# Eight shifted copies of 64 lags for the Toeplitz rows, and blocks of q*v 56 rows apart

## The chip, the core and the metric

The kernel is one program on one core of a Trainium2 chip. Its time is the device time of one execution in microseconds (us), and lower is better. The core has five engines that take instructions in order, each from a list of its own: TensorE (PE in the profile, with its weight loads as PEld), VectorE (DVE), ScalarE (ACT), GpSimd (POOL) and SyncE (SP), which here issues transfers only. Sixteen DMA engines move data between device memory (HBM) and the on-chip SBUF. A transfer is issued by an instruction on SP, ACT or POOL and runs beside the computation.

## The reference

The input is `x`, 8 images of 56 x 56 positions with 192 channels, float32. Four layers each add something to it. Layers 0 and 1 are the ones that the change touches:

```python
p = silu(x @ p_w.T + p_b)          # x after a group norm; D1 = 576 channels
q = silu(x @ q_w.T + q_b)
v = silu(x @ v_w.T + v_b)
qv = q * v
o1 = _toeplitz(qv.reshape(b * h, w, D1), a1)     # along the rows
o2 = _toeplitz(transpose(qv), a2)                # along the columns
out = (p * (o1 + o2)) @ o_w.T + o_b
```

`_toeplitz` multiplies every line of 56 positions, channel by channel, with a 56 x 56 Toeplitz matrix, whose 111 coefficients (one for each lag) come from a small network of the lag times a decay that depends on the channel. Layer 2 is a ConvNeXt block and layer 3 is attention in windows; the change leaves both alone.

## The kernel before, in words

**Passes.** The images are handled in pairs and fours: `qvs` holds two HBM tensors, one for images 0, 1 and 4, 5 and one for the rest. For each layer and each of them there is a q/v pass (`tno_qv`, called Q: normalise on ACT at L246, 128 x 256 matmuls at L263, bias add on VectorE at L272, SiLU on ACT at L301, product on GpSimd at L304, store of the product to `qv` by SP at L307), a Toeplitz pass (`tno_toeplitz`, called TZ) and an output pass (`tno_out`, called O: loads of the sums `s` at L508 and of `x` at L119, matmuls at L536 to L592).

**Layout of qv.** A block holds 32 channels of four images: 56 x 56 positions with 128 values each, the four images of a channel side by side. Before the change a block has room for 64 rows of 56 positions; the last 8 rows are zeros, written once by two transfers of GpSimd's queue at L743.

**Coefficient tables.** `decay_tables` (L136) works out the 111 coefficients of each channel, in chunks of 128 channels. For each chunk a tile `a` (L191) holds them in reverse order with zeros behind, and SP writes them to an HBM table as shifted copies (L204): row g of the table holds, for 32 channels, the lags from 4g on. With `TG, TW = 16, 60` there are 16 such copies of 60 lags. A Toeplitz step reads its coefficient tile `tm` from them with four transfers (L393), each filling every fourth partition: partition 4g + k gets the g-th copy shifted by k more. That yields 64 partitions for each of the two blocks of the step, each shifted by one lag from the one above. The matmul then takes 32 consecutive lags as its weights.

**Toeplitz steps.** Each TZ runs 18 steps n, in pairs: `blk, d = divmod(n, 2)`. A step works on two blocks (64 channels), along rows where d is 0 and along columns where d is 1. Its `q` tile is 128 partitions of 56 x 128 values, two buffers. For d = 0 it comes by two transfers (L380) that put the position within the row on the partitions, one of them on ACT's queue; for d = 1 it comes by one transfer (L383), which takes 128 rows of 28672 bytes as they stand, the rows of zeros among them. The matmuls of L406 use 56 partitions of each half. ACT copies the results out (L413), VectorE transposes and adds (L424, L426), GpSimd adds (L429) and stores sums of finished blocks (L436, L444). The loads of step n + 2 are issued after the last group of step n.

**Order of the work.** `tno_layers` (L681) starts with a table stage, in which the statistics of the input, the first Q and the tables of both layers alternate. Then four TZ passes follow, each woven by `weave` (L644) with a lane of Q and O work: whenever the lane has done its share, the next part of a TZ step is issued. PE, ACT, DVE and POOL run in the order in which the program is written; the order on SP's queue is set by the framework. `tm` has two tiles, the products that wait to be stored have three buffers (`tp`, `bufs=3`), and `x` tiles of `input_stats` have seven (L215).

Of the kernel before, what the change touches and what calls it, by code (L numbers as in the profile page):

```python
# [12 lines left out]
F32 = mybir.dt.float32  # L13
# [13 lines left out]
B, H, W, C = 8, 56, 56, 192  # L27
T = H * W
HALF = [slice(0, 64), slice(64, 128)]
TT = 448  # L30
NT = T // TT
D1 = 576
# [6 lines left out]
def view(ap, offset, dims):  # L39

    return bass.AP(ap.tensor, ap.offset + offset, [ap.ap[0], *dims])


class Net:
# [86 lines left out]

    TG, TW = 16, 60

    def decay_tables(self, L, p, tables):  # L136

        nc, inp = self.nc, self.inp
        tv = p.tile([32, 111], F32, name=f"{L}tv", bufs=1)
        nc.sync.dma_start(tv, inp["tvec"])  # L140
        pows = []
        for c in range(5):
            m = min(128, D1 - 128 * c)
            sl = p.tile([128, 1], F32, name=f"{L}sl")
            nc.sync.dma_start(sl[:m], inp[f"{L}_slope"][128 * c : 128 * c + m, :])
            nc.vector.tensor_scalar(sl[:m], sl[:m], 0.0, 1.0, ALU.max, ALU.min)
            nc.vector.tensor_scalar(sl[:m], sl[:m], 1.0 - 0.95, 0.95, ALU.mult, ALU.add)
            pw = p.tile([128, 64], F32, name=f"{L}pw", bufs=5)
            nc.gpsimd.memset(pw[:m, 0:1], 1.0)
            n = 1  # L150
            while n < 64:
                nc.vector.tensor_scalar(
                    pw[:m, n : 2 * n], pw[:m, 0:n], sl[:m], None, ALU.mult
                )
                n *= 2
                if n < 64:
                    sq = p.tile([128, 1], F32, name=f"{L}sl")
                    nc.vector.tensor_mul(sq[:m], sl[:m], sl[:m])
                    sl = sq
            pows.append(pw)  # L160
            yield 1.0
        for d in range(2):
            t = f"{L}_t{d + 1}"
            w0 = p.tile([32, 2], F32, name="w0")
            nc.sync.dma_start(w0[:, 0:1], inp[f"{t}_w0"])
            nc.sync.dma_start(w0[:, 1:2], inp[f"{t}_b0"])
            ws = p.tile([32, 3, 32], F32, name="ws")
            nc.sync.dma_start(ws, inp[f"{t}_ws"])
            bs = p.tile([32, 3], F32, name="bs")
            nc.sync.dma_start(bs, inp[f"{t}_bs"])  # L170
            wo = p.tile([32, D1], F32, name="wo")
            nc.sync.dma_start(wo, inp[f"{t}_wo"])
            bo = p.tile([128, 5], F32, name="bo")
            nc.sync.dma_start(bo, inp[f"{t}_bo"])
            h = p.tile([32, 111], F32, name=f"{L}h")
            nc.vector.tensor_scalar(h, tv, w0[:, 0:1], w0[:, 1:2], ALU.mult, ALU.add)
            nc.vector.tensor_scalar(h, h, 0.0, None, ALU.max)
            for i in range(3):
                hp = self.bank2()[:32, 0, :111]
                nc.tensor.matmul(hp, ws[:, i, :], h, start=True, stop=True)  # L180
                h = p.tile([32, 111], F32, name=f"{L}h")
                nc.vector.tensor_scalar(h, hp, bs[:, i : i + 1], 0.0, ALU.add, ALU.max)
                yield 1.0
            for c in range(5):
                m = min(128, D1 - 128 * c)
                ap = self.bank2()[:, 0, :111]
                nc.tensor.matmul(
                    ap[:m], wo[:, 128 * c : 128 * c + m], h, start=True, stop=True
                )
                a = p.tile([128, 4 * self.TG + 56], F32, name=f"{L}a")  # L190
                nc.gpsimd.memset(a[:m, 111:], 0.0)  # L191
                back = view(pows[c][:m], 55, [[-1, 55]])
                for lo, hi, dec in ((0, 55, back), (55, 111, pows[c][:m, 0:56])):
                    nc.vector.scalar_tensor_tensor(
                        view(a[:m], 110 - lo, [[-1, hi - lo]]),
                        ap[:m, lo:hi],
                        bo[:m, c : c + 1],
                        dec,
                        ALU.add,
                        ALU.mult,  # L200
                    )
                for n in range(m // 32):
                    to = tables[d][self.TG * (4 * c + n) : self.TG * (4 * c + n + 1)]
                    nc.sync.dma_start(  # L204
                        to.rearrange("g (c w) -> c g w", w=self.TW),
                        view(a[32 * n : 32 * n + 32], 0, [[4, self.TG], [1, self.TW]]),
                    )
                yield 1.0

    def input_stats(self, xs, gn, j, p):  # L210

        nc = self.nc
        st = self.tp.tile([128, 3, 14, 6], F32, name="st", bufs=2)
        for t in range(NT):
            x = p.tile([128, 3, TT], F32, name="x", bufs=7)  # L215
            self.load_pair(x, xs, j, slice(t * TT, (t + 1) * TT))
            for k in range(3):
                nc.vector.bn_stats(st[:, k, t, :], x[:, k, :])
            yield
        self.norms.append(self.pair_gn_finish(st[:, :, :NT], gn, j))  # L220
        for more in self.all_norms():
            pass

    def tno_qv(self, L, j0, xs, gn, qv, apart=None, cols=(0, 2 * D1), g0=0):
# [3 lines left out]
        nc, p, inp = self.nc, self.tp, self.inp  # L228
# [5 lines left out]
        w, bias = self.wq[:, 0:2], self.wq[:, 2]  # L234
# [62 lines left out]
        def multiply(m, n, z, at, c0):  # L297
            k = n // 128
            for f in stores:
                f()  # L300
            nc.scalar.activation(z[:m, :n, :], z[:m, :n, :], AF.Silu)  # L301
            prod = p.tile([128, 4, DC * 4], F32, name="t4")
            half = z[:m, :n, :].rearrange("p (n h c) b -> p n h (c b)", h=2, c=DC)
            nc.gpsimd.tensor_mul(prod[:m, :k], half[:, :, 0], half[:, :, 1])  # L304
            n0 = c0 // 128
            stores[:] = [
                lambda: nc.sync.dma_start(  # L307
                    qv[2 * n0 : 2 * n0 + 2 * k, at : at + m, :].rearrange("n t e -> t n e"),
                    prod[:m, :k].rearrange("p n (h e) -> p (n h) e", h=2),
                )  # L310
            ]
# [7 lines left out]
        if apart:  # L319
            units = []  # L320
            for g in range(2):
                x, t0, n = loaded[g]
                for s in range(0, n, 128):
                    for c0 in range(0, 2 * D1, 512):
                        k = min(512, 2 * D1 - c0)
# [19 lines left out]
        for g in range(2 if apart else g0, groups):  # L345
            x, t0, n = loaded.pop(0)
# [18 lines left out]
    def tno_toeplitz(self, j0, mats, qv, o):  # L365
# [6 lines left out]
        def load(n):  # L372
            blk, d = divmod(n, 2)
            q = p.tile([128, H, 128], F32, name="q", bufs=2)
            if d == 0:

                for half in range(2):
                    of = qv[2 * blk + half, :T].rearrange("(h w) e -> w h e", w=W)
                    by = nc.scalar if half and n > 1 else nc.sync
                    by.dma_start(q[64 * half : 64 * half + W], of)  # L380
            else:
                of = qv[2 * blk : 2 * blk + 2].rearrange("n (h w) e -> (n h) (w e)", w=W)
                nc.sync.dma_start(q.rearrange("p i e -> p (i e)"), of)  # L383
            return q

        def matrices(n):

            blk, d = divmod(n, 2)
            row = 32 * self.TW
            at = mats[d].offset + 2 * blk * self.TG * row  # L390
            for k in range(4):
                of = bass.AP(mats[d].tensor, at + k, [[row, 2 * self.TG], [1, row]])
                nc.sync.dma_start(self.tms[n % 2][k:128:4], of)  # L393

        def along(n, q, ot, g):
# [285 lines left out]
    def tno_layers(self, x0, x1, x2, gn, last):  # L681
# [11 lines left out]
        ]  # L693
        qvs = {

            j0: self.dram.tile([D1 // 32, 64 * W, 128], F32, name=f"qv{j0}") for j0 in (0, 2)
        }
        o = [self.dram.tile([B // 2, 9, 128, T], F32, name=f"{L}_sum") for L in LS]
        x = (x0, x1, x2)
        with ExitStack() as ctx, ExitStack() as wqp:  # L700
# [7 lines left out]
            with tc.tile_pool(name="tab", bufs=2) as tab:  # L708
# [20 lines left out]
                with tc.manual_schedule(engines=ENGINES):  # L729
                    for n in range(28):  # L730
                        next(more, None)
                        if n == 18:
                            next(rest)
                        if next(first, None) is None:
                            next(rest)
                        if n < 21:
                            next(decay[0])
                        if n >= 7:
                            next(decay[1])
                        if n in (14, 21):  # L740
                            qv = qvs[0 if n == 14 else 2]
                            to = qv[:, T:].rearrange("n (p k) e -> p n (k e)", p=112)
                            nc.gpsimd.dma_start(to, view(none, 0, [[0, D1 // 32], [1, 512]]))  # L743
                    for more in decay:
                        assert next(more, None) is None
                lanes = [[(rest, QT * 5 / 9 * 21 / 25 - 25.0), (Q(0, 2), QT)], [(O(0, 0), OT), (Q(1, 0), QT)]]
# [933 lines left out]
```

## Time and profile before

| | us |
|---|---|
| median of 3 runs | 5438.96 |
| lowest and highest run | 5432.41, 5443.45 |
| profiled execution, device time | 5425.63 |
| its span | 5423.8 |
| TensorE busy in the span | 5166.0 (95%) |
| VectorE busy | 2589.3 (48%) |
| ScalarE busy | 2383.5 (44%) |
| GpSimd busy | 1767.2 (33%) |

The median is the time that is compared. All durations below come from the one profiled execution. Its span runs from the first to the last recorded instruction; 1.8 us of its device time lie around the span. Busy shares are averages over the whole span. The table stage lasts from about 100 to 376 us, the woven stages from 376 to about 2970 us, and the later layers follow. A row of a timeline gives the start, the duration, the engine, the line, the operation, the target and source tiles by name, and in brackets the idle time before it and what ended it. In a list of waits each line gives the waiting engine and line, what it waited for, and then total us, times, and the longest.

### The profile page before, as it was taken

How to read it: one execution, taken by the hardware profiler on the slowest of the kernel's cores; microseconds unless marked ns; L12 is line 12 of the kernel's file. 1: busy time of each engine (PE TensorE's matmuls, PEld its weight loads, DVE VectorE, ACT ScalarE, POOL GpSimd, SP SyncE). 2: the span in 40 equal slices, each digit the busy share in tenths (PEclk: the TensorE clock that was granted, in tenths of full speed). 3: DMA queues.
4: the chain of work that ended last, by engine and by line, in shares of the span. 5: the costliest groups of instructions: out<-in, count | busy, mean ns of one | idle time of the engine just before them, and what ended most of it. 6: DMA issues, size and time to landing. Idle time of an engine off the chain costs nothing.

```text
span 5423.8 us, 144350 instructions
## 1 busy us (share of the span) xinstructions
PE 5166.0 (95%) x64672; PEld 3811.2 (70%) x64672; DVE 2589.3 (48%) x3990; ACT 2383.5 (44%) x3179; POOL 1767.2 (33%) x1291
## 2 busy tenths in 40 slices
PE   7879999999999999999999899989999999999998
PEld 4657777777777777777777789856665444777776
DVE  6535556455555555555556422422222331566666
ACT  3345555444554454655455422243323333444443
POOL 2225675133664243546443100000000100333333
PEclk9889999999999999999999999999999999999998
DMA  7699997888786999889897667635454221445552
GB/s 251 151 243 283 289 311 234 265 281 267 241 262 176 307 317 318 279 226 291 285 312 266 205 223 248 229 96 190 135 174 124 75 68 49 85 98 108 101 102 68
DMA packets 1051146, 1116.48 MB, mean 206 GB/s; under 512 B 235200, under 2 KB 986304, under 8 KB 1036128
## 3 DMA queue, kind: packets, MB, share of 16 engines
q1 hardware_dynamic: 911584, 854.88, 52.9%
q0 software_dynamic: 38144, 200.99, 9.6%
q10 hardware_dynamic: 100800, 51.38, 3.9%
q8 instruction: 508, 8.32, 0.6%
q14 instruction: 110, 0.90, 0.1%
HBM read 743.17 MB, written 363.94 MB: 204 GB/s over the span
## 4 chain that ended last, share of the span: by engine, by line
PE 50%; DVE 3%; DMA 3%; issue 1%; ACT 1%; POOL 1%; SPq 0%; POOLq 0%; ACTq 0%; DVEq 0%
PE bank L980 7%; PE bank L837 5%; PE bank L1060 5%; PE bank L1254 4%; PE bank L263 4%; PE bank L592 3%; PE bank L1074 3%; PE bank L536 3%; PE bank L1370 2%; PE bank L1201 2%; PE bank L1284 2%; PE bank L1325 2%; PE bank L406 2%; PE bank L586 1%; PE bank L1344 1%
## 5 line engine op out<-in xcount | busy, mean ns | idle before, releaser
L263 PE MATMUL bank<-wq,t 128*128 128x256 f32 (+4 forms) x7680 | 1290.3, 374 | 72.1 <-DVE t L272 40.8
L263 PEld LDWEIGHTS bank<-wq,t 128*128 128x128 f32 (+2 forms) x7680 | 1005.2, 190 | 350.8 <-issue 92.4
L272 DVE TENSOR_TENSOR t<-bank,wq 128x1024 f32<-128x1024 f32 (+3 forms) x480 | 517.7, 1112 | 692.5 <-PE bank L263 537.1
L304 POOL TENSOR_TENSOR t<-t 128x1024 f32<-128x1024 f32 (+2 forms) x288 | 528.0, 1847 | 676.5 <-ACT t L301 339.1
L413 ACT COPY ot<-bank 128x896 f32<-128x896 f32 x576 | 493.4, 909 | 515.1 <-PE bank L406 401.8
L429 POOL TENSOR_TENSOR s<-s,ot 128x1568 f32<-128x1568 f32 x128 | 551.1, 4306 | 193.8 <-DVE ot L426 128.4
L301 ACT ACTIVATE t<-t 128x2048 f32<-128x2048 f32 (+2 forms) x288 | 423.0, 1488 | 328.8 <-DVE t L272 319.0
L406 PE MATMUL bank<-q,tm 56*32 56x224 f32 x18432 | 504.9, 353 | 22.0 <-DMA tm<-L_tab 10.6
L406 PEld LDWEIGHTS bank<-q,tm 56*32 56x32 f32 x18432 | 340.0, 106 | 148.2 <-issue 81.7
L122 POOL DMA_DIRECT2D x<-t x112 | 87.0, 777 | 1071.7 <-DVE t L601 1007.4
L560 DVE TENSOR_TENSOR t<-t,bank 128x896 f32<-128x896 f32 x224 | 242.8, 1088 | 401.6 <-ACT bank L555 346.0
L555 ACT ACTIVATE bank<-bank,wo 128x448 f32<-128x448 f32 x448 | 262.8, 605 | 377.4 <-PE bank L545 349.8
L980 PE MATMUL bank<-z,w 128*128 128x448 f32 (+1 forms) x1344 | 413.3, 555 | 2.8 <-DVE xt L828 2.8
L536 PE MATMUL bank<-t,wo 128*128 128x224 f32 x1792 | 375.9, 364 | 21.1 <-ACT t L515 10.6
L536 PEld LDWEIGHTS bank<-t,wo 128*128 128x128 f32 x1792 | 337.7, 194 | 51.7 <-issue 29.6
L592 PE MATMUL bank<-t,wo 128*128 128x224 f32 x1792 | 368.9, 359 | 0.0
L592 PEld LDWEIGHTS bank<-t,wo 128*128 128x128 f32 x1792 | 329.9, 190 | 31.1 <-issue 31.1
L980 PEld LDWEIGHTS bank<-z,w 128*128 128x128 f32 (+1 forms) x1344 | 183.0, 189 | 209.8 <-issue 199.5
L837 PEld LDWEIGHTS bank<-xt,cm 113*112 113x112 f32 x3072 | 309.7, 178 | 25.7 <-issue 23.3
L837 PE MATMUL bank<-xt,cm 113*112 113x108 f32 (+2 forms) x3072 | 316.0, 263 | 1.0 <-ACT h L989 1.0
L127 POOL DMA_DIRECT2D x<-x x64 | 36.7, 573 | 855.5 <-DVE x L1011 796.7
L424 DVE STREAM_TRANSPOSE s<-ot 128x1792 f32<-128x1792 f32 x144 | 292.8, 2034 | 24.5 <-ACT ot L413 16.2
(162 smaller groups left out, 6977.2 us busy)
## 6 DMA issues: line engine op xcount, KB each, us to landing
q<-qv SPq DMA_DIRECT2D x36, 3584.0 KB
t<-L_sum SPq DMA_DIRECT2D x112, 1008.0 KB
L_sum<-s POOLq DMA_DIRECT2D x256, 392.0 KB, 7.2
qv<-t SPq DMA_DIRECT2D x192, 512.0 KB
cm<-in_L_cm SPq DMA_DIRECT2D x96, 896.0 KB
tm<-L_tab SPq DMA_DIRECT2D x288, 240.0 KB
q<-qv SPq DMA_DIRECT2D x40, 1568.0 KB
q<-qv ACTq DMA_DIRECT2D x32, 1568.0 KB
```

The source lines that it names most:

```text
L263: nc.tensor.matmul(pp[:m, b, 256 * j : 256 * j + k], x[rows, j, 2 if part else b, s : s + m], w[rows, part, c0 + c : c0 + c + k],  start=p ...
L272: nc.vector.tensor_add(z[:m, c : c + k, :], view(pp[:m], 0, [[1, k], [256, 4]]), view(bias[:m], c0 + c, [[1, k], [0, 4]]),)
L301: nc.scalar.activation(z[:m, :n, :], z[:m, :n, :], AF.Silu)
L304: nc.gpsimd.tensor_mul(prod[:m, :k], half[:, :, 0], half[:, :, 1])
L406: nc.tensor.matmul(pt[32 * j : 32 * j + 32, r, hf * 224 : (hf + 1) * 224], tm[rows, at : at + 32], q[rows, :, 4 * c : 4 * c + 4], start=Tr ...
L413: nc.scalar.copy(view(ot, 4 * (g % 4), [[16, 2], [32, 112], [1, 4]]), view(pt, 0, [[512, 2], [4, 112], [1, 4]]),)
L424: nc.vector.transpose(to, of.rearrange("p (i k) -> p i k", k=32))
L429: add.tensor_add(to, to, view(of, 0, [[1, 28], [32, 56]]))
L536: mm(gs[c // 2][:, b, c % 2 * 256 : c % 2 * 256 + N], pw[:, 0, 128 * c : 128 * c + 128], xn[:, b], start=c % 2 == 0, stop=False,)
L592: mm(P[:, b, :N], ow[:, c, 0:128], g[:, 4 * b + c], start=False, stop=c == 3)
L837: nc.tensor.matmul(pc[:, 128 * e + 4 * m0 : 128 * e + 4 * m1], cm[:113, e, k, :], xt[:, m0 - 1 + k : m1 - 1 + k, c + e, :], start=n == 0 a ...
L980: nc.tensor.matmul(phs[c][:, s, :TT], w0[rows, part, at : at + 128], z[rows, Z[2 if part else s], :], start=part == flip, stop=part != flip,)
```

## The change

The table keeps 8 copies of 64 lags, each shifted by 8, where it kept 16 of 60, shifted by 4. A `tm` tile takes 8 table rows for each 32 channels, and each twice: once from its start and once from 4 lags on, hence `[4, 2]` in the source of L392. The coefficient tiles `a` stay 120 wide (4 x 16 + 56 and 8 x 8 + 56) and have four buffers in place of two. Blocks of `qv` stand 56 rows apart, with no zeros between them; 8 rows of zeros stand at the end of each of the two tensors, since the load of the last block also takes 64 rows. The d = 1 load reads, for each of two blocks that begin 56 rows apart, 64 rows. What it reads beyond 56 isn't used by the matmuls. The `x` tiles of `input_stats` have six buffers in place of seven.

```diff
-    TG, TW = 16, 60
+    TG, TW = 8, 64
...
-                a = p.tile([128, 4 * self.TG + 56], F32, name=f"{L}a")
+                a = p.tile([128, 8 * self.TG + 56], F32, name=f"{L}a", bufs=4)
...
-                        view(a[32 * n : 32 * n + 32], 0, [[4, self.TG], [1, self.TW]]),
+                        view(a[32 * n : 32 * n + 32], 0, [[8, self.TG], [1, self.TW]]),
...
-            x = p.tile([128, 3, TT], F32, name="x", bufs=7)
+            x = p.tile([128, 3, TT], F32, name="x", bufs=6)
...
-                    qv[2 * n0 : 2 * n0 + 2 * k, at : at + m, :].rearrange("n t e -> t n e"),
+                    qv[2 * n0 * T : 2 * (n0 + k) * T].rearrange("(n t) e -> t n e", t=T)[at : at + m],
...
-                    of = qv[2 * blk + half, :T].rearrange("(h w) e -> w h e", w=W)
+                    of = qv[(2 * blk + half) * T :][:T].rearrange("(h w) e -> w h e", w=W)
...
-                of = qv[2 * blk : 2 * blk + 2].rearrange("n (h w) e -> (n h) (w e)", w=W)
+                rows = qv.rearrange("(h w) e -> h (w e)", w=W)[2 * H * blk : 2 * H * blk + H + 64]
+                of = bass.AP(rows.tensor, rows.offset, [[H * W * 128, 2], [W * 128, 64], [1, W * 128]])
...
-                of = bass.AP(mats[d].tensor, at + k, [[row, 2 * self.TG], [1, row]])
+                of = bass.AP(mats[d].tensor, at + k, [[row, 2 * self.TG], [4, 2], [1, row]])
...
-            j0: self.dram.tile([D1 // 32, 64 * W, 128], F32, name=f"qv{j0}") for j0 in (0, 2)
+            j0: self.dram.tile([D1 // 32 * T + 8 * W, 128], F32, name=f"qv{j0}") for j0 in (0, 2)
...
-                            to = qv[:, T:].rearrange("n (p k) e -> p n (k e)", p=112)
-                            nc.gpsimd.dma_start(to, view(none, 0, [[0, D1 // 32], [1, 512]]))
+                            to = qv[D1 // 32 * T :].rearrange("(p k) e -> p (k e)", p=112)
+                            nc.gpsimd.dma_start(to, none)
```

## The prediction

> **What bounds the kernel now.** I read the page's busy shares first, then the waits, then windows of the woven stages, then timelines around single loads. The page:
> ```profile
> span 5423.8 us, 144350 instructions
> PE 5166.0 (95%) x64672; PEld 3811.2 (70%) x64672; DVE 2589.3 (48%) x3990; ACT 2383.5 (44%) x3179; POOL 1767.2 (33%) x1291
> q<-qv SPq DMA_DIRECT2D x36, 3584.0 KB
> tm<-L_tab SPq DMA_DIRECT2D x288, 240.0 KB
> ```
> TensorE is busy for 95% of the span. It is the bound, and a transfer costs time only where TensorE comes to wait for it. The one large transfer that the change rewrites is the `q<-qv` load of L383: 36 of 3584 KB each, on SP's queue.
>
> The list of waits (total, times, longest) says what such loads cost now:
> ```profile
> POOL t L304 <- DMA qv<-t: 306.1, 54, 31.1
> ...
> PE bank L406 <- DMA tm<-L_tab: 10.6, 1, 10.6
> ...
> PE bank L406 <- DMA q<-qv: 3.4, 1, 3.4
> ```
> TensorE waits once for a coefficient tile and once for a `q` tile: both kinds of load are hidden. GpSimd's products already wait 306.1 us for stores of `qv`, so SP's queue is not idle.
>
> Windows: busy time of PE, PEld, DVE, ACT, POOL, then granted clock, mean busy share of the 16 DMA engines, GB/s. In order: all woven stages; the start of one L383 load; the start of the next; attention's `v` loads of L1233; the last `v` load of L1240 alone:
> ```profile
> 376.00:2970.00 2594.00, 2500.34 (x31566) 1945.96 (x31566) 1421.15 (x1393) 1354.29 (x1840) 1233.35 (x764) 0.98 0.86 275
> 1066.00:1075.00 9.00, 8.96 (x125) 6.52 (x124) 5.48 (x4) 5.45 (x9) 7.25 (x6) 1.00 1.06 418
> 1136.00:1145.00 9.00, 8.90 (x125) 6.47 (x124) 5.82 (x4) 4.58 (x8) 7.09 (x6) 1.00 1.09 425
> 4617.50:4618.30 0.80, 0.80 (x24) 0.65 (x16) 0.23 (x1) 0.48 (x1) 0.00 (x0) 1.00 1.02 161
> 4619.10:4619.45 0.35, 0.35 (x20) 0.07 (x8) 0.00 (x0) 0.00 (x0) 0.00 (x0) 1.00 0.21 33
> ```
> The DMA engines are 86% busy over the woven stages. The L383 load, whose source is 128 equal rows, keeps all 16 busy at 418 to 425 GB/s, 26.1 to 26.6 GB/s for each. The last two rows matter most. L1233's source has a leading count of 48 and its loads fill all engines (1.02). L1240's has a leading count of 4 and holds a share of 0.21, 3.4 engines of 16, for the whole 0.35 us. Spread over 16 engines the same packet time would be over in 0.35 x 0.21 = 0.07 us.
>
> Timeline of SP's queue, with the two L383 loads of the rows above, then of TensorE, with the first use of the first of them and two groups of 32 matmuls in the table stage:
> ```profile
> 1065.05 0.44 SPq L383 DMA_DIRECT2D q<-qv  x1
> ...
> 1098.85 0.34 SPq L380 DMA_DIRECT2D q<-qv  x1
> ...
> 1134.80 0.33 SPq L383 DMA_DIRECT2D q<-qv  x1
> ```
> ```profile
> 211.26 0.54 PE L180 MATMUL bank<-L1h,ws 32*32 32x111 f32 x2 [9.74 <-DVE L1h L177]
> 211.74 8.48 PE L263 MATMUL bank<-wq,t 128*128 128x256 f32 x32
> ...
> 282.86 0.54 PE L180 MATMUL bank<-L1h,ws 32*32 32x111 f32 x2 [7.50 <-issue]
> ...
> 294.12 5.65 PE L263 MATMUL bank<-wq,t 128*128 128x256 f32 x32
> ...
> 313.06 3.35 PE L263 MATMUL bank<-wq,t 128*128 128x256 f32 x7 [10.76 <-ACT t L246]
> ...
> 1105.18 1.75 PE L406 MATMUL bank<-q,tm 56*32 56x224 f32 x64
> ```
> A load issued at 1065.05 is used at 1105.18, 40.1 us later. 29.6 us after that the next is issued. The 36 loads start from 369.2 to 2903.3 us, so one pair of steps takes (2903.3 - 369.2)/35 = 72.4 us.
>
> **The change, part by part.**
>
> *The load of L383 (after: L382 to L384).* Without rows of zeros the two blocks of a pair lie 56 rows apart, and the kernel reads 64 rows from each. This can't be one run of 128 rows any more. The source becomes [2][64 rows][28672 bytes]: leading count 2 in place of 128. Bytes and packet size stay. No trace of before has a leading count of 2 at this size. The nearest rows bound it: 16 engines (L383 as it is) and 2 engines (L1240's row, taken to mean that no more engines serve a load than its leading count). L1240's is the only source here with a count below 16 that runs alone, so I take 2. It differs in that its target is a single partition, which is why I keep the other end.
>
> On 2 engines: 3.67 MB / 2 / 26.35 GB/s = 70 us per load on each, against some 9 us on 16. Other queues, not served behind SP's, take part of them (packets, MB, share of 16 engines in the woven stages):
> ```profile
> q0 software_dynamic: 22944, 139.60, 13.5%
> q10 hardware_dynamic: 100800, 51.38, 8.1%
> ```
> That is 0.22 x 72.4 = 16 us of each period, a third of it in the stretch in question: 5 us. Landing comes 75 us after issue.
>
> What waits behind it: SP's queue is served in order on each engine, so the two engines' shares of the `tm` loads, the `s` and `x` loads and the stores of `qv` issued afterwards all land after the large load. TensorE therefore stops before it even needs `q`. Beside TNO output stages (O) the `s` loads run two tiles of 13 us ahead, so work goes on for about 33 us (first `s` load behind the large one at 1077.5, used some 22 us on). Beside the q/v stages (Q) three buffers hold products, whose stores no longer land: three groups of 5.65 us, about 17 us. O and Q cover about half of the steps each: 25 us on average. So TensorE loses 75 - 25 = 50 us per load, 36 x 50 = 1800 us. Bounds: no engine can do better than its own work, 70 us plus the rest of its work per pair. The share of 0.86 x 72.4 = 62 us has some 9 to 10 us of the large load in it, so 70 + 52 = 122, or 44 where `qv` stores and zeros weigh least: 112 - 72 = 40 us per load, +1440. At the other end nothing overlaps: 36 x 75 = +2700.
>
> After each long stop TensorE restarts at a lower clock: the 32 matmuls after the 9.74 us gap took 8.48 us, undisturbed ones 5.65. 36 x 2.5 = +90 us (0 to 36 x 5).
>
> [...]
>
> *Table stage (100 to 400 us).* Coefficient tiles have four buffers, the descriptors of table writes halve (512 pieces of 240 B per write become 256 of 256 B), and the zero fill (2 x 4032 KB, 18.7 us each to land) shrinks to 2 x 224 KB. The gap of 9.74 us before 211.26 holds a 5.47 us wait of VectorE for `L1sl`, whose load stands behind table writes on SP; that load now stands ahead of them: -5.5. The gap of 7.50 us at 282.86 comes from `L0a` buffers: -6. The gap of 10.76 us at 313.06 follows an `in_x` load that stands behind fills and stores on full engines (with the clock after it): -12. `tm` at 376: -2. One `x` buffer less at the start: +0 to +2. Sum -25, with bounds -38 (all gaps) and +2 (none, cover gone).
>
> *Edits at nothing.* The `tm` load is 256 KB in place of 240: 288 x 16 KB = 4.7 MB, 0.2 us per step at 275 GB/s, hidden by 72 us of matmuls per pair. Its source leads with 16, as many as the engines. The `qv` stores write the same bytes, and the order of instructions on the compute engines is the same but for two tiny VectorE moves. The L380 load keeps its 56 leading rows.
>
> **Sum.** The profiled execution took 5425.63 us (span 5423.8 and 1.8 around it), 13.3 under the median of 5438.96. 5425.6 + 1800 + 90 - 25 = 7291, and on the median's footing 7304; I say 7300.
>
> **Rivals.**
> 1. *Well hidden, same cause.* Loads only fill the two engines' idle time: +1440 - 25, 6854. For: share 0.86 leaves these engines little slack either way. Against: products have three buffers, `q` two, so TensorE can't run far ahead.
> 2. *No overlap.* TensorE stops almost at each issue: +2700 + 90 - 25, 8204. For: the 306.1 us of waits for `qv` stores show how little room there is. Against: 40.1 us from issue to first use.
> 3. *The other side, faster.* The load still spreads over 16 engines and lands in 9 us: only the table stage's -25 stays, 5414. It decides from 4 engines up: 3.67 MB / 4 / 26.35 = 35 us, under the 40.1 that are there. For: L1240's target is one partition, so its share might come from there. Against: one partition would give one engine, not 3.4.
> 4. *No change:* 16 engines, and the table stage's gain goes into the next wait there: 5439.
>
> **How the numbers follow.** Main case 0.60, rival 1 0.16, rival 2 0.15, rival 3 0.07, rival 4 0.02. A change under 0.2% (11 us) is about what a measurement of this kernel can't tell from none. Faster 0.07, same 0.02, slower 0.91. The range leaves out rivals 3 and 4 and the far end of rival 2: 6700 (floor with nothing lost to restarts and a somewhat smaller share of other work) to 8150.
>
> **What would show it.** Right: L406 waits for `q<-qv` or L272/L304/L560 wait for stores and `s` loads, tens of us, once per large load; the DMA share in the woven stages falls from 0.86 to about half, GB/s with it; two thirds to one half busy TensorE there, its granted clock below 0.98 after each stop; a window with the large load alone at a share near 2/16 = 0.13 and some 53 GB/s. In the table stage the gaps at 282 and 313 are gone. Wrong: 400 GB/s after an issue of L384, no new waits in the woven stages. The size fails if packets of the two engines run faster than 26 GB/s when the other 14 are idle, or if work goes on for more or less than 25 us behind a load.

## The result, and the profile after

| | before | after |
|---|---|---|
| median | 5437.93 us (4 runs, 5432.41 to 5443.45) | 7609.99 us (4 runs, 7600.44 to 7621.78) |
| ratio | 1 | 1.3995, 95% interval 1.397 to 1.402 |
| span of the profiled execution | 5423.8 us | 7611.5 us |

The changed kernel is 40% slower. 7300 us was predicted, with a range of 6700 to 8150.

The page of the changed kernel:

```profile
span 7611.5 us, 144319 instructions
PE 5316.2 (70%) x64672; PEld 3891.5 (51%) x64672; DVE 2591.2 (34%) x3990; ACT 2388.8 (31%) x3179; POOL 1764.4 (23%) x1291
q<-qv SPq DMA_DIRECT2D x36, 3584.0 KB
tm<-L_tab SPq DMA_DIRECT2D x288, 256.0 KB
L_sum<-s POOLq DMA_DIRECT2D x256, 392.0 KB, 17.1
```

The work is the same: as many matmuls and the same loads, each `tm` load 16 KB larger. TensorE is busy 70% of the span in place of 95%. Even GpSimd's stores of sums, which are on another queue, take 17.1 us to land (median) where they took 7.2. The row of the kernel before:

```profile
L_sum<-s POOLq DMA_DIRECT2D x256, 392.0 KB, 7.2
```

The list of waits (total, times, longest), and below it the row for sums in the kernel before:

```profile
POOL t L304 <- DMA qv<-t: 1417.5, 72, 94.9
DVE t L272 <- POOL t L304: 1109.2, 53, 87.8
...
PE bank L407 <- DMA tm<-L_tab: 772.2, 17, 59.6
...
DVE t L561 <- DMA t<-L_sum: 691.5, 14, 66.7
...
PE bank L407 <- DMA q<-qv: 3.0, 1, 3.0
```

```profile
DVE t L560 <- DMA t<-L_sum: 48.6, 5, 12.8
```

TensorE's new waits are nearly all booked to what stands behind the large load on SP's queue: coefficient tiles (L407, 10.6 us before), sums (L561, 48.6 us before), and stores of products (L304, 306.1 us before), which stop VectorE and then TensorE. The 3.0 us for `q` itself mislead. The list books a wait to what came last, and the four `tm` loads of a step are issued right behind its `q`. In 17 of the 36 loads the long stop of TensorE ends at the first matmul that uses this load's `q`, 3.1 to 6.2 us after the load's last packet; 16 of these stops are booked to `tm` (756.7 of the 772.2 us). There TensorE had come to the use of `q` itself. In the other 19 it stops earlier, for stores and sums.

One load as an example, from SP's timeline and TensorE's:

```profile
1329.26 0.53 SPq L384 DMA_DIRECT2D q<-qv  x1
1329.84 8.51 SPq L394 DMA_DIRECT2D tm<-L_tab  x4
1338.80 68.87 SPq L307 DMA_DIRECT2D qv<-t  x2
```

```profile
1359.33 7.80 PE L263 MATMUL bank<-wq,t 128*128 128x256 f32 x32
1412.26 3.24 PE L407 MATMUL bank<-q,tm 56*32 56x224 f32 x64 [45.13 <-DMA tm<-L_tab]
```

The load is issued at 1329.26 and TensorE goes on until about 1367. SP itself stands still for most of 68.87 us within a pair of stores: the issue of one alone takes 63.9. The load's last packet ends at 1409.1, and TensorE resumes at 1412.26, with the first matmul that uses this `q`. The windows in between (busy PE, PEld, DVE, ACT, POOL, granted clock, DMA share, GB/s), with the stretch from the first issue of L384 to the last as the last row:

```profile
1370.00:1380.00 10.00, 0.00 (x0) 0.00 (x0) 0.00 (x0) 0.00 (x0) 0.00 (x0) 0.53 0.12 52
...
1390.00:1400.00 10.00, 0.00 (x0) 0.00 (x0) 0.00 (x0) 0.00 (x0) 0.00 (x0) 0.50 0.12 52
...
347.70:5024.30 4676.60, 2579.53 (x30673) 1972.94 (x30674) 1381.95 (x1346) 1324.01 (x1784) 1211.36 (x748) 0.77 0.51 150
```

All five engines stand still, and the DMA engines show a share of 0.12 at 52 GB/s: 2 of 16, at 26 GB/s each. The granted clock falls to 0.50. The same stretch in the kernel before:

```profile
369.20:2903.30 2534.10, 2434.21 (x30673) 1893.86 (x30674) 1380.25 (x1346) 1319.41 (x1784) 1212.19 (x748) 0.98 0.86 276
```

The same instructions took 2534.10 us and now take 4676.60. For each of the 35 periods that is 72.4 and 133.6 us, 61.2 more. TensorE's idle part went from (2534.10 - 2434.21)/35 = 2.9 us to 59.9, and its busy part, at a lower clock, from 69.5 to 73.7.

### The profile page after: what moved, and what is told of

Its sections match the earlier page's. It is cut to its first block, busy times and chain, and to the rows that moved or that the text cites. A ratio compares the mean times of both kernels' runs of the same rounds, so it can differ in the third digit from the quotient of the medians.

```text
span 7611.5 us, 144319 instructions
## 1 busy us (share of the span) xinstructions
PE 5316.2 (70%) x64672; PEld 3891.5 (51%) x64672; DVE 2591.2 (34%) x3990; ACT 2388.8 (31%) x3179; POOL 1764.4 (23%) x1291
## 3 DMA queue, kind: packets, MB, share of 16 engines
q10 hardware_dynamic: 100800, 51.38, 3.3%
## 5 line engine op out<-in xcount | busy, mean ns | idle before, releaser
L263 PE MATMUL bank<-wq,t 128*128 128x256 f32 (+4 forms) x7680 | 1343.3, 384 | 515.3 <-DVE t L272 419.9
L263 PEld LDWEIGHTS bank<-wq,t 128*128 128x128 f32 (+2 forms) x7680 | 1043.6, 196 | 814.5 <-DVE t L272 459.1
L407 PE MATMUL bank<-q,tm 56*32 56x224 f32 x18432 | 547.0, 373 | 1074.2 <-DMA tm<-L_tab 772.2
L407 PEld LDWEIGHTS bank<-q,tm 56*32 56x32 f32 x18432 | 351.3, 111 | 1222.9 <-issue 580.5
L304 POOL TENSOR_TENSOR t<-t 128x1024 f32<-128x1024 f32 (+2 forms) x288 | 526.8, 1842 | 1780.7 <-DMA qv<-t 1415.1
L561 DVE TENSOR_TENSOR t<-t,bank 128x896 f32<-128x896 f32 x224 | 241.4, 1087 | 1285.3 <-DMA t<-L_sum 691.5
L537 PE MATMUL bank<-t,wo 128*128 128x224 f32 x1792 | 396.4, 376 | 154.4 <-DVE t L602 73.5
L593 PE MATMUL bank<-t,wo 128*128 128x224 f32 x1792 | 368.9, 359 | 0.0
L576 PE MATMUL bank<-t,wo 64*64 64x224 f32 x448 | 74.2, 401 | 385.8 <-DVE t L561 376.6
L427 DVE STREAM_TRANSPOSE ot<-ot 128x1792 f32<-128x1792 f32 x144 | 292.4, 2033 | 0.0
## 6 DMA issues: line engine op xcount, KB each, us to landing
L_sum<-s POOLq DMA_DIRECT2D x256, 392.0 KB, 17.1
```

Source lines behind the costliest of these rows:

```text
L263: nc.tensor.matmul(pp[:m, b, 256 * j : 256 * j + k], x[rows, j, 2 if part else b, s : s + m], w[rows, part, c0 + c : c0 + c + k],  start=p ...
L407: nc.tensor.matmul(pt[32 * j : 32 * j + 32, r, hf * 224 : (hf + 1) * 224], tm[rows, at : at + 32], q[rows, :, 4 * c : 4 * c + 4], start=Tr ...
L537: mm(gs[c // 2][:, b, c % 2 * 256 : c % 2 * 256 + N], pw[:, 0, 128 * c : 128 * c + 128], xn[:, b], start=c % 2 == 0, stop=False,)
L593: mm(P[:, b, :N], ow[:, c, 0:128], g[:, 4 * b + c], start=False, stop=c == 3)
```

## The experiments

Theory A is the prediction's: the leading count of a transfer's source sets how many DMA engines serve it. Rival B: the new layout or table costs the time. Theory C came up on the way. This table holds all kernels; the first two number columns come from the trace's packet records (the 28672-byte packets of the large load), the period from the first packets of its first and last load.

| kernel | median packet, us | first to last packet of a load, mean, us | period, us | time, us |
|---|---|---|---|---|
| before | 1.07 | 12.0 | 72.4 | 5438 |
| after | 1.06 | 79.1 | 133.5 | 7610 |
| before_count2 | 1.06 | 78.8 | 132.0 | 7578 |
| count4 | 1.68 | 66.9 | 122.7 | 7222 |
| count8 | 1.86 | 38.3 | 96.4 | 6269 |
| count16 | 2.04 | 19.4 | 80.5 | 5703 |
| two_loads | 2.06 | 20.4 | 79.8 | 5680 |
| before_halves | 2.05 | 20.0 | 79.2 | 5680 |
| old_fill | 2.06 | 20.5 | 79.7 | 5682 |
| two_queues | 2.03 | 21.2 | 80.1 | 5680 |
| two_queues_56 | 1.96 | 19.7 | 78.4 | 5632 |
| old_layout | 1.07 | 12.2 | 73.1 | 5436 |
| act_queue | 1.06 | 83.5 | 136.9 | 7715 |
| same_half | 1.58 | 116.7 | 171.6 | 8918 |

### Is it the leading count?

```diff
 # before_count2: before, L383
-of = qv[2 * blk : 2 * blk + 2].rearrange("n (h w) e -> (n h) (w e)", w=W)
+rows = qv[2 * blk : 2 * blk + 2].rearrange("n (h w) e -> (n h) (w e)", w=W)
+of = bass.AP(rows.tensor, rows.offset, [[63 * W * 128, 2], [W * 128, 64], [1, W * 128]])
```

> The kernel before with one edit: the source of L383 is written as 2 blocks of 64 rows whose starts are 63 rows apart, in place of 128 rows; the second block of each pair so lands one row off, and the output isn't the reference's. Bytes and packet sizes are those of before. Theory A: 2 engines, the period of a pair of steps grows from 72 to about 134 us as in the changed kernel, and with no gain in the table stage the time is 5438 + 36 x 61 = about 7630 us (7500 to 7750). Rival B: layout and tables are those of before, so about 5438 us.

Measured: 7578.22 us, ratio 1.3928 (1.3903 to 1.3954). Only the way the source is written differs from before, and nearly the whole loss is there. Theory A holds; rival B is out as its main cause. The packet records of the runs with 4, 8 and 16 pieces below say the same: the time that a load's packets took, divided by the load's length, gives 1.8 packets under way at once in the changed kernel, 3.3 with 4 pieces, 6.7 with 8 and 13.2 with 16, where the kernel before has 13.0.

```diff
 # two_loads: after, L384
-of = bass.AP(rows.tensor, rows.offset, [[H * W * 128, 2], [W * 128, 64], [1, W * 128]])
-nc.sync.dma_start(q.rearrange("p i e -> p (i e)"), of)
+for r in range(2):
+    of = rows[H * r : H * r + 64]
+    nc.sync.dma_start(q.rearrange("p i e -> p (i e)")[64 * r : 64 * r + 64], of)
```

> The changed kernel with one edit: the load of L384 is two transfers of 64 rows each, so the leading count of each source is 64; bytes, layout, rows and everything else of the change stay. Theory A (the leading count sets how many DMA engines serve a load): both transfers use all 16 engines, the waits of the woven stages vanish, and the table stage's gain of 20 to 28 us is left: 5410 to 5420 us, a share near 1 right after the issue. Rival B (the new layout costs the time: blocks 56 rows apart, the eight overlapping rows read twice, or the new coefficient table): the two transfers read the same rows, so the time stays above 7000 us.

Measured: 5680.03 us, ratio 1.0438 (1.0419 to 1.0457). Nine tenths of the loss are gone, which neither theory gave: A said 5415, B over 7000. The windows of two_loads show why A fell short, both in the first load, the first row as it begins:

```profile
353.00:361.00 8.00, 0.35 (x9) 0.26 (x17) 0.00 (x0) 0.00 (x0) 0.00 (x0) 0.50 1.12 204
360.00:368.00 8.00, 7.35 (x147) 5.16 (x148) 0.00 (x0) 4.78 (x5) 0.00 (x0) 0.73 0.98 205
```

All 16 engines are busy (1.12, 0.98), but at 205 GB/s, where the one load of 128 rows had 418 to 425 at a share of 1.06 to 1.09. Each packet takes 2.06 us in place of 1.07.

```diff
 # count4, count8, count16: after, L384
-[[H * W * 128, 2], [W * 128, 64], [1, W * 128]]
+[[28 * W * 128, 4], [W * 128, 32], [1, W * 128]]    # count4
+[[14 * W * 128, 8], [W * 128, 16], [1, W * 128]]    # count8
+[[7 * W * 128, 16], [W * 128, 8], [1, W * 128]]     # count16
```

> The changed kernel with the source of L384 written as 4 pieces of 32 rows, 28 rows apart: leading count 4, the same bytes in the same number of packets. Rows land in other partitions, so the output isn't the reference's. Theory A with the prediction's account of what stands behind the load (work goes on for 25 us after the issue): 4 engines, 32 packets of 1.06 us and 6 us of other work on each, landing 43 us after the issue, so TensorE loses 18 us per load and 2 to 3 us of lower clock: 5414 + 36 x 20 = about 6150 us (5950 to 6300). Theory A with the bound that the prediction gave in its third rival (only the use of q counts, 40.1 us after the issue): at most 3 us per load, 5414 to 5530 us. Rival B: about 7600 us, as the pieces overlap here too.

> As the run with 4 pieces, with 8 pieces of 16 rows, 14 rows apart; the output isn't the reference's either. Theory A: 8 engines, 16 packets of 1.06 us and 3 us of other work, landing 23 us after the issue, within the 25 us that work goes on: 5414 to 5450 us, hardly above the kernel with two transfers of 64 rows. If work stops earlier than 25 us in part of the woven stages, some 5 us of that show per load: up to 5600 us. Rival B: about 7600 us.

Measured: 7221.55 us (ratio 1.3273, 1.3246 to 1.3299) and 6269.26 us (1.1518, 1.1498 to 1.1538). Both are far above what theory A gave, 6150 and at most 5600. Twice the engines did not halve the load: its packets grew to 1.68 and 1.86 us. The count matters, but something else does too.

### What makes packets longer?

Packets take 2.06 us with two transfers of 64 rows, 1.68 with 4 pieces and 1.86 with 8, where they take 1.07 in the kernel before and 1.06 in the changed one. Theory C is a guess from these lengths: besides the number of engines, it counts which partitions are written at the same time. two_loads writes 64 of them with each transfer; the pieces of one load start 64 partitions apart in the changed kernel, 32 apart in count4 and 16 apart in count8. No trace here names the engine or the partition of a packet; what the runs can show is how long packets get.

> The changed kernel with the source of L384 written as 16 pieces of 8 rows, 7 rows apart (leading count 16, one transfer to all 128 partitions); rows land in other partitions, so the output isn't the reference's. [...] Theory A alone (only the count of engines matters): 5405 to 5430 us.

Measured: 5702.92 us, ratio 1.0487 (1.0473 to 1.0501); packets of 2.04 us. One transfer to all 128 partitions still passes data at about half the rate when it is cut into 16 pieces of 8 neighbours: 19.4 us for a load, against 12.0 before. So it isn't the number of partitions of a transfer; that it is which of them are written at once is theory C's account, which this run doesn't contradict.

```diff
 # two_queues: two_loads, the second half on ACT's queue; two_queues_56: with 56 rows and no fill
-nc.sync.dma_start(q.rearrange("p i e -> p (i e)")[64 * r : 64 * r + 64], of)
+by = nc.scalar if r and n > 1 else nc.sync
+by.dma_start(q.rearrange("p i e -> p (i e)")[64 * r : 64 * r + 64], of)
```

> The kernel with two transfers of 64 rows, the second of them issued on ACT's queue in place of SP's (as the kernel does for the load of L380), so that both are under way together; the first two steps of each pass stay on SP. Theory C, if the engines mix packets of both queues: all 128 partitions are being written at once, packets come down from 2.06 to 1.1 to 1.4 us, both halves land in 12 to 15 us, and the time is 5410 to 5450 us. Rival, that two such transfers simply follow each other on the same 16 engines however they are issued: packets stay near 2.06 us, both land after 20 us, 5650 to 5700 us.

> As the run with two queues, but only the 56 rows that are used are read for each block, so no rows of zeros and no fill are needed at all. The leading count is 56, which 14 of 16 engines can share evenly. Bytes fall by an eighth. If packets mix (theory C): 5405 to 5445 us, within 0.3% of the run with 64 rows, as 14 engines x 56 rows take as long as 16 x 64. If they don't: 5650 to 5700 us, as with one queue.

Measured: 5679.74 us (1.0444, 1.043 to 1.0459) and 5632.16 us (1.035, 1.0329 to 1.0372). I had hoped that packets of the two queues would mix. In 16 of the 32 loads that two_queues splits, one half has landed before the other begins, or within 1.1 us after, so there was nothing to mix. In the other 16 the halves run side by side for 5 to 16 us, and packets are hardly shorter: 1.94 us, the load 18.3 us long. An eighth less data gives some 48 us. That 14 engines serve 56 rows is an estimate and not shown for this run; in the kernel before, the 32 loads of 56 rows on ACT's queue (L380) take 100800 packets, for each load 3136 of 512 bytes and 14 of 4 bytes.

```diff
 # same_half: after, L384
-of = bass.AP(rows.tensor, rows.offset, [[H * W * 128, 2], [W * 128, 64], [1, W * 128]])
-nc.sync.dma_start(q.rearrange("p i e -> p (i e)"), of)
+for r in range(2):
+    of = bass.AP(rows.tensor, rows.offset + r * H * W * 128,
+                 [[28 * W * 128, 2], [W * 128, 32], [1, W * 128]])
+    nc.sync.dma_start(q.rearrange("p i e -> p (i e)")[64 * r : 64 * r + 64], of)
```

> The changed kernel with its load of L384 as two transfers, one for each half of the partitions, each of 2 pieces of 32 rows, 28 rows apart: leading count 2, so two engines serve all of it as in the changed kernel, but now they write partitions 32 apart at the same time, where in the changed kernel they lie 64 apart. The output isn't the reference's. [...] Rival (packets were long in the runs with 4, 8 and 16 pieces because many engines were at work at once): 1.06 us as in the changed kernel, 7560 to 7650 us.

Measured: 8918.16 us, ratio 1.6409 (1.6269 to 1.6548). Two pieces at a time, as in the changed kernel, but 32 partitions apart, and the load takes 116.7 us in place of 79.1, with packets of 1.58 us in place of 1.06 as the median. By these figures some 1.7 packets (128 x 1.58 / 116.7) were under way at once, an estimate, against 1.8 in the changed kernel. So it isn't the number of busy engines. Packets go up and down, mostly between 1.06 and 2.26 us; why they do isn't known. What stays open: the pieces also lie 28 rows apart in HBM rather than 56, and no run moves the partitions alone. The runs with two halves weaken this rival: each half reads 64 rows that stand one after another, with no pieces 28 rows apart, and packets are as long (2.05 and 2.06 us).

```diff
 # before_halves: before, L383
+for r in range(2):
+    half = slice(64 * r, 64 * r + 64)
-nc.sync.dma_start(q.rearrange("p i e -> p (i e)"), of)
+    nc.sync.dma_start(q.rearrange("p i e -> p (i e)")[half], of[half])
```

> The kernel before with one edit: the load of L383 is two transfers of 64 rows, to partitions 0 to 63 and 64 to 127; the layout, the rows of zeros, the tables and everything else are those of before. [...] Theory B (blocks 56 rows apart cost something by themselves, and that is what slowed the kernel with two transfers): 5437 to 5450 us, packets of 1.07 us.

Measured: 5679.71 us, ratio 1.0438 (1.0419 to 1.0458). Two halves cost 240 us in the old layout as well. A load of 20 us fits well into the time before its use, 28.5 to 57.2 us after the issue in the kernel before, but for 8 us more per pair all 16 engines are taken (shares of 0.96, 1.08 and 1.03 in windows of 10 us within three loads). The stretch from its first large load to its last:

```profile
373.10:3146.30 2773.20, 2510.29 (x30676) 1934.18 (x30677) 1377.17 (x1348) 1322.89 (x1785) 1212.39 (x749) 0.95 0.89 252
```

The DMA engines were busy for 0.86 x 72.4 = 62 us of each period and now are for 0.89 x 79.2 = 70. The period grows by 6.8 us: TensorE is idle for 4.7 us more of it, and its busy part is 2.2 us longer, at a granted clock of 0.95 in place of 0.98. That the fuller DMA engines cause these stops is argued from this sum, not shown.

### What is the rest of the change worth?

before_halves and two_loads differ by everything else of the change, and their medians are 5679.71 and 5680.03 us. That is nothing, where the prediction had a gain of 25. before_count2 and after are another such pair, with the load on two engines, and there the rest goes with a loss: 7578.22 against 7609.99 us, 32 us, and the intervals of their ratios don't overlap. But before_count2 has two executions only, and its blocks start 63 rows apart and not 56. Which of the differences costs the 32 us isn't known.

```diff
 # old_fill: two_loads, at the place of the fill
+big = self.dram.tile([D1 // 32, 64 * W, 128], F32, name=f"big{n}")
+to = big[:, T:].rearrange("n (p k) e -> p n (k e)", p=112)
+nc.gpsimd.dma_start(to, view(none, 0, [[0, D1 // 32], [1, 512]]))
 # old_layout: before with TG, TW = 8, 64, [8, ...] in L206, [4, 2] in L392,
 # bufs=4 for the tile of L190 and bufs=6 for that of L215
```

> The changed kernel with two transfers of 64 rows (5680 us) plus the fill of before: two transfers of 4032 KB of zeros on GpSimd's queue at the places where before writes its rows of zeros, to a tensor that nothing reads. By the prediction the fill is worth 12 us (the gap at 313 us and the clock behind it): 5690 to 5695 us. If the fill is hidden, or what it delays is given back later: 5675 to 5685 us.

> The kernel before with the rest of the change: 8 copies of 64 lags, four buffers for the coefficient tiles, six for x; blocks of qv stay 64 rows apart with their rows of zeros, so the load of L383 is one transfer of 128 rows. By the prediction's terms the wait for L1sl and the gap of L0a go (5.5 + 6 us), while the zero fill stays with its 12 us: 5421 to 5432 us. If the table's gain comes from the fill alone: 5436 to 5442 us. If the 256-byte pieces or the pairs of reads at an offset of 4 lags cost something in the woven stages: above 5445 us.

Measured: old_fill 5681.88 us (ratio 1.0451, 1.0426 to 1.0476), the same as without; old_layout 5435.6 us, ratio 0.9995 (0.9986 to 1.0004), no difference that can be measured. The table stage did become shorter. In the changed kernel's timeline the gaps of 9.74, 7.50 and 10.76 us shrink or are gone:

```profile
206.34 0.35 PE L180 MATMUL bank<-L1h,ws 32*32 32x111 f32 x2 [4.72 <-DVE L1h L177]
...
272.46 8.50 PE L263 MATMUL bank<-wq,t 128*128 128x256 f32 x32 [1.26 <-ACT t L246]
...
299.45 5.65 PE L263 MATMUL bank<-wq,t 128*128 128x256 f32 x32
...
305.36 15.00 PE L263 MATMUL bank<-wq,t 128*128 128x128 f32 x97
```

and the first large load is issued at 347.7 us in place of 369.2. But it doesn't last. In the profiled executions the first load of two_loads is issued 25.3 us ahead of that of before_halves, the 25th still 18.9, the 30th 0.7. The first load of old_layout is issued 11.4 us ahead of before's, the 8th 0.7 behind it; the first load of after 23.1 us ahead of that of before_count2, the last 33.1 behind. The woven stages take longer by as much or more. Which wait gives it back isn't settled.

### What stops TensorE before the load has landed?

```diff
 # act_queue: after, L384
-nc.sync.dma_start(q.rearrange("p i e -> p (i e)"), of)
+nc.scalar.dma_start(q.rearrange("p i e -> p (i e)"), of)
```

> The changed kernel with its load of L384 (leading count 2, one transfer) issued on ACT's queue in place of SP's. It tells what stops TensorE some 25 us after the issue. If it is only the order within SP's queue (stores, sums and coefficient tiles stand behind 64 large packets on two engines), these now pass, and TensorE loses time only when it needs the q tile itself: 82 - 40 = 42 us per load in place of 57, so 7610 - 36 x 15 = about 7070 us. If the two engines take packets of both queues in turn, small ones wait for a large one each (72 pieces of 896 bytes per engine for one load of sums, against 64 packets of 1.06 us), and nothing is won: 7450 to 7700 us. If the issue also holds up ACT: above 7700 us.

Measured: 7714.51 us, ratio 1.4183 (1.4143 to 1.4222). Its waits:

```profile
POOL t L304 <- DMA qv<-t: 1480.7, 70, 70.4
...
DVE t L561 <- DMA t<-L_sum: 718.6, 16, 74.5
...
PE bank L407 <- DMA q<-qv: 327.7, 6, 74.0
```

The stores and sums on SP's queue are as late as in the changed kernel although the large load is on another. So it isn't the order within a queue alone: products wait for their stores for 1480.7 us, against 1417.5 in the changed kernel, and for sums VectorE waits 718.6 us against 691.5. That small pieces hardly get past the large packets of the other queue on the two engines, as in the second case of the expectation, fits these waits and isn't shown packet by packet. The time lies above that case's range, where the third case has an issue that holds up ACT; but the issue takes ACT 0.5 us (median, at most 1.1), so ACT isn't held up. The load itself lands later, 86.1 us after its issue on average against 82.2. TensorE's waits for `tm` are gone from the list and 327.7 us are booked to `q`, since `q` now lands after `tm`: in 11 of the 36 loads the long stop ends at the use of `q`.

## Why the prediction was right, and where it was off

- **The load on 2 engines** was right, and with it the sign and the scale. L1240's share of 0.21 with a leading count of 4 was the row that told it; the target of one partition, the reason for keeping the other end, did not matter. The windows of the changed kernel, 0.12 and 52 GB/s, show the 0.13 and 53 GB/s that were named as a sign.
- **What waits behind it** was right in part. Stores and sums do stop TensorE, but "before it even needs `q`" holds for 19 loads of 36; in the other 17 it stops at the use of `q`. The order of SP's queue on each engine was given as the reason. The packet records fit it: of the 128 packets of the four `tm` loads behind a large load, 16 (median of 36 loads), two sixteenths, begin only in the last 1.1 us of that load or after it; in the kernel before, with all 16 engines on the load, 128 (also the median). But act_queue shows that another queue doesn't help.
- **The work behind a load** was put at 25 us and measures 31: so long TensorE is busy on average between the issue and the landing. Beside O it is 31.9 us, where 33 were taken, but beside Q 29.5, where the three product buffers were to give 17.
- **The landing time** was put at 75 us and measures 82.2. 64 packets of 1.064 us are 68, close to the 70 taken; longer packets and the gaps between them add 11, where 5 were taken for other transfers; and the first packet begins 3.1 us after the issue, for which nothing was taken.
- **The loss per load** was put at 75 - 25 = 50 us and measures 57 (idle time of 59.9 us per period less 2.9). The two misses above nearly cancel, as 82.2 - 31 = 51, and that is luck. What the sum lacks is the time from the landing to the end of the stop, until what stands behind the load has landed too: 5.6 us on average. In all 36 x 7 = 250 us.
- **The clock** was taken as 2.5 us per load and cost 73.7 - 69.5 = 4.2, another 60 us.
- **The table stage's -25** was right as a local change (21.5 us at the first load) and wrong in the sum: it is given back later, in the changed kernel perhaps with 32 us on top. Without the -25, 7300 + 250 + 60 + 25 = 7635 us, against 7610.
- **The third rival's threshold**, "it decides from 4 engines up", was wrong. It counted engines and the use of `q` alone, and took that from one load: the uses come 28.5 to 57.2 us after the issue, 37.4 on average. Four pieces gave 7222 us, and loads that keep all sixteen engines busy at half the rate 5680 to 5703.
- **The period in the first rival**, 112 to 122 us, was meant as a floor; the period measured is 133.6, as TensorE worked only some 31 us on behind each load. Its sum slips: 70 + 44 is 114, not 112. And its other end, 122 - 72 = 50 us, is the main case's own loss per load, so it bounded nothing there.

## What to carry to other kernels

When a transfer's pattern is rewritten, look at its slowest dimension before its bytes: here the same bytes in the same packets took 79 us in place of 12, since that dimension went from 128 to 2. One transfer over all 128 partitions whose slowest dimension is the partitions themselves took 12.0 to 12.2 us; every other arrangement tried, in halves, in pieces or over two queues, 19.4 us or more. Rows of zeros that let two blocks be read as one uniform run were worth 194 us here against the fastest arrangement without them (two_queues_56), and some 240 against the others in halves; leaving out their fill gained nothing measurable. And a wait is booked to what landed last: before calling a load hidden, look at what landed just ahead of it.

## What the runs showed of the hardware that was not expected

- 16 busy DMA engines moved 205 GB/s or 420, by how the load was cut: packets of 28672 bytes took 2.04 to 2.06 us or 1.07. That the partitions written together decide it is theory C; it fits the runs, which don't separate it from where the rows lie in HBM.
- Two pieces at a time, 32 partitions apart (and 28 rows apart in HBM), took between 1.06 and about 2.26 us per packet, 1.58 as the median; with pieces 64 partitions apart the median stayed at 1.06.
- Issuing halves from two queues changed nothing in the time (5679.74 and 5680.03 us), though in half of the loads the halves ran side by side.
- A large load on two engines delays small transfers of other queues too: GpSimd's stores of sums landed after 17.1 us in place of 7.2 (from 400 to 2900 us 15.1 in place of 7.1, and 13.6 in two_loads, with two halves on all engines).
